# Feed-forward weights loaded a step ahead and let through by TensorE's progress, row norms from the accumulators, tiles of their own in the first batch

## The chip, the cores and the metric

The program runs on one core of one Trainium2 chip. The metric is device microseconds (us) of one execution, lower is better. Before the change three runs took 1228.06, 1234.43 and 1236.42 us, so the median is 1234.43 us.

Engines in the profile: PE is TensorE's matmul stream, PEld its weight loads, DVE is VectorE, ACT ScalarE, POOL GpSimd, SP SyncE. SP and POOL issue the kernel's DMAs. Each engine takes its own instructions strictly in order, so an instruction that waits holds up all that stand behind it on its engine.

## The reference

One decoder layer on x of 4 x 512 x 512 (batch, tokens, features) in float32:

```python
q = (ln(x) @ Wq + bq).reshape(B, T, 128, 16)   # k and v alike
att = softmax(q^T k / sqrt(128))               # per head 128 x 128: tokens are summed over
y = (att @ v).reshape(B, 512, 2048) @ Wo + bo  # per head 128 x 512
x = x + y
x = x + gamma * xattn(ln(x), ctx, ctx)         # 8 heads of 64 features, softmax over 512
w = clip(round(w / mean|w|), -1, 1) * mean|w|  # for w1, w3, w2 (1365 x 512)
x = x + (silu(ln(x) @ w1^T) * (ln(x) @ w3^T)) @ w2^T
```

Weights come as kernel inputs, so the quantization to three values is part of the computation: the mean of the absolute values of a whole matrix has to be known before any entry of it can be rounded.

## The kernel before, in words

**Attention, four rounds a batch.** Because an attention matrix sums over tokens, the kernel forms the Gram matrix `G = xn^T xn` of a batch once (`gram_upper`, `gram_rest`; matmuls `pg`, `gt`), and then runs rounds j = 0 to 3, each of four heads g = 0 to 3. A round has four products of 512 x 512 x 512: u = xn · Wo_j (matmuls `pu`), y = G · Wk_j (`py`), m = Wv_j · u (`pm`) and the scores Wq_j · y (`sc`). After them come the softmax `e` (`scores`: reduce_max L437, L438, exp L442, scaling L453), its transpose (`turned`, matmuls `pe`) and the output (`output`, matmuls `po`), which adds into four accumulators `acc` of 128 x 512 (L468). The transpose and output of a round are issued in the middle of the next one. All matmuls write into eight banks of PSUM, handed out in turn: a bank is used again only when what reads it (the exp for a score bank) is done.

**The first batch** also prepares the weights. `first_weights` loads four raw chunks of 128 x 512 for each of o, k, v, q, subtracts the last row (L227) and adds the bias by a small DMA on POOL (L230). `keep_weights` splits a chunk into parts h, l and, in later rounds, d (L253, L255, L258) and stores them to DRAM from POOL (L244). The raw chunks of o and q share seven buffers (tag "raw"), those of k and v and the parts of o share the 18 tiles of pool `a_w`, and the parts of k and v share twelve (tag "part"). The scaling at L227 multiplies by `gate`, a value that is always 1.0 but is computed from a result of TensorE (`gate_of`, L208): it has no effect on the numbers and makes the instruction depend on that result. The kernel is put in order by a scheduler that works from priorities and its own estimates; a gate keeps it from placing an instruction too early in an engine's order. Batches 1 to 3 load the kept parts (`weights`; for batch 1, d of the early rounds is made at L273) into pool `a_w`.

**Beside batches 1 to 3** run two side jobs, advanced by `tick()` inside `products`: `quantize` goes over w1, w3 and w2 in pieces (12, 12 and 11), first summing absolute values (`abs_w`, L498), then comparing with the scale (`tern_w`, L521, L522) and storing to DRAM on SP's queue (L525); both passes load a piece through `staged` (two buffers) right before they use it. `cross(b - 1)` is the cross-attention of the batch before: it loads the rows of x_a (the stored accumulators) once for the row norms (`cs`, L550, L551) and once more for the work (`cx`, L558), then scores `xs`, softmax, transposes `xp`, and `xo`. The cross-attention of batch 3 runs beside the feed-forward part, with its DMAs on POOL's queue.

**The feed-forward part** (L836 on) is one dense stream of matmuls with the quantized weights resident.

What the change and the steps of the prediction touch are the pools (L133 to L137, L747 to L751), `first_weights`, `keep_weights`, `weights`, the gates (L709, L720, L726), `held` (L738 to L740), `staged`, `quantize_steps` and the head of `cross`.

Of the kernel before, what the change touches and what calls it, by code (L numbers as in the profile page):

```python
# [10 lines left out]
F32 = mybir.dt.float32  # L11
# [7 lines left out]
P = 128  # L19
# [18 lines left out]
def decoder_layer_kernel(  # L38
# [29 lines left out]
    x_a = [dram.tile([T, D], F32, name=f"x_a_{b}") for b in range(B)]  # L68
    x_c = [dram.tile([T, D], F32, name=f"x_c_{b}") for b in range(B)]

    kept_t = {
# [58 lines left out]
    def apool(name, bufs):  # L130
        return apools.enter_context(tc.tile_pool(name=name, bufs=bufs))

    x3p, xnp, g3p, u3p, wp = (  # L133
        apool("a_x3", 12), apool("a_xn", 4), apool("a_g3", 1), apool("a_u3", 12), apool("a_w", 18)
    )
    yp, stp, tp = apool("a_y", 5), apool("a_stage", 2), apool("a_t", 3)
    ep, mp, accp = apool("a_e", 1), apool("a_m", 4), apool("a_acc", 4)  # L137
# [43 lines left out]

    def wtile(name, dt=F32R):
        return wp.tile([P, GW], dt, tag="w", name=name)

    w_of = {"q": wq, "k": wk, "v": wv}
# [25 lines left out]
    def first_weights(n, j, first, gate):  # L211

        if n != "o":
            last = first.tile([P, GW], F32, tag="last", bufs=2, name=f"{n}_last_{j}")
            load(heads(last), of_heads(w_of[n][:, D - 1 : D, :], j).to_broadcast([P, NG, DH]))
        chunks = []
        for k in range(KC):
            name = f"{n}_raw_{j}_{k}"
            if n in "oq":
                t = first.tile([P, GW], F32, tag="raw", bufs=7, name=name)  # L220
            else:
                t = wtile(name, F32)
            if n == "o":
                load(t, by_group(wo[j * T : (j + 1) * T, :], k))
            else:
                load(heads(t), of_heads(w_of[n][:, ts(k, P), :], j))
                nc.vector.scalar_tensor_tensor(t, t, gate[0], last, ALU.mult, ALU.subtract)  # L227
                if k == KC - 1:
                    bias = bqkv[:, ts(KINDS.index(n), GW)].rearrange("(o g) c -> g o c", o=1)
                    nc.gpsimd.dma_start(heads(t[P - 1 :, :]), of_heads(bias, j))  # L230
            chunks.append(t)
        return chunks

    def keep_weights(n, j, chunks, first, gate):


        def part(p, k):
            name = f"{n}_{p}_{j}_{k}"
            if n == "o":
                return wtile(name)  # L240
            return first.tile([P, GW], F32R, tag="part", bufs=12, name=name)

# [19 lines left out]

    def weights(n, b, j):
        if n == "q":
            return [load(wtile(f"q_{b}_{j}_{k}", F32), kept_q[j][ts(k, P), :]) for k in range(KC)]
        tris = []
        for k in range(KC):
            tri = Tri(*(wtile(f"{n}{p}_{b}_{j}_{k}") for p in "hld"))
            make = b == 1 and not exact(n, 0, j)
            for p in "hl" if make else "hld":  # L270
                load(getattr(tri, p).bitcast(F32), kept[n, j, p][ts(k, P), :])
            if make:
                nc.vector.tensor_tensor(  # L273
                    tri.d, tri.l.bitcast(F32), tri.h.bitcast(F32), ALU.subtract
                )
                nc.gpsimd.dma_start(kept[n, j, "d"][ts(k, P), :], tri.d.bitcast(F32))
            tris.append(tri)
        return tris

    def products(name, lhs, rhs, done, tick):  # L280

        for pair in ((0, 1), (2, 3)):
# [19 lines left out]
            for i in pair:  # L302
                done(i, hs[i], pd[i])
            tick()

# [165 lines left out]


    third = (HID + 2) // 3

# [9 lines left out]
    def staged(src, name):  # L484
        r, n = src.shape
        return load(stp.tile([P, 512], F32, tag="stage", name=name)[:r, :n], src)

    def quantize_steps(name):

# [5 lines left out]
        nc.vector.memset(sums, 0.0)  # L495
        for i, (src, t) in enumerate(pieces):
            piece = staged(src, f"abs_{name}_{i}")
            nc.vector.tensor_reduce(  # L498
# [17 lines left out]
        yield  # L516
        for i, (src, t) in enumerate(pieces):
            piece = staged(src, f"tern_{name}_{i}")
            r, n = t.shape
            above = stp.tile([P, 512], BF16, tag="above", name=f"above_{name}_{i}")  # L520
            nc.vector.tensor_scalar(above[:r, :n], piece, s[:r, 0:1], None, ALU.is_gt)  # L521
            nc.vector.scalar_tensor_tensor(  # L522
                piece, piece, s[:r, 1:2], above[:r, :n], ALU.is_lt, ALU.subtract
            )
            load(t, piece)  # L525
            yield
# [8 lines left out]
    xscale = 1.0 / math.sqrt(XD)  # L535
    CROSS_STEPS = 2 * NC + 1 + NC * (2 * NC + 2)

    def cross(b, cx, cin, cpp, cpt):
# [6 lines left out]

        mv = small.tile([P, NC, 2], F32, tag="mvc", bufs=2, name=f"mv_c_{b}")
        for c in range(NC):
            yield
            yield
            t = load(cx.tile([P, D], F32, tag="x", name=f"cs_{b}_{c}"), x_a[b][ts(c, P), :])  # L550
            moments(mv[:, c, :], t, f"c_{b}_{c}")  # L551
        rstd = small.tile([P, NC], F32, tag="rstdc", bufs=2, name=f"rstd_cc_{b}")
        nc.vector.tensor_copy(rstd, rstd_of(mv, f"c_{b}"))
        yield
# [116 lines left out]
    for j in range(HG):  # L671
# [30 lines left out]
        else:  # L702
# [46 lines left out]
        cpools.enter_context(tc.tile_pool(name=n, bufs=k, side="right"))  # L749
        for n, k in (("c_x", 3), ("c_in", 2), ("c_p", 4), ("c_pt", 2))  # L750
    ]  # L751
    for b in range(1, B):
        G = gram_upper(b, xs)
        waiting[2] = turned(*waiting[:3])
        output(*waiting)
        side = Side(cross(b - 1, *cpool), CROSS_STEPS, TICKS + 6)

# [5 lines left out]
        for j in range(HG):  # L763
            u3 = values_out(b, j, x3, weights("o", b, j), tick)
            if j > 0:
                waiting[2] = turned(*waiting[:3])
            ys = keys_of(b, j, g3, weights("k", b, j), tick)
            if j > 0:
# [6 lines left out]
            ms = values_of(b, j, weights("v", b, j), u3, tick)  # L775
            e = scores(b, j, weights("q", b, j), ys)
            waiting = [b, j, e, ms, accs]
        side.rest()
    waiting[2] = turned(*waiting[:3])
    output(*waiting)  # L780
    quant.rest()
    apools.close()

# [152 lines left out]
```

## Time and profile before

| | us |
|---|---|
| median of three runs | 1234.43 |
| the profiled execution | 1231.67 |
| its span in the profile | 1229.4 |
| PE busy | 1184.3 (96%) |
| DVE busy | 777.5 (63%) |
| ACT busy | 448.5 (36%) |
| POOL busy | 140.9 (11%) |
| DMA moved | 257.20 MB, mean 209 GB/s |

The profiled execution took 2.3 us more than its span; what lies around the span is not in the trace. Busy is time in which an engine had an instruction under way. Idle time of PE is therefore 1229.4 - 1184.3 = 45.1 us in all. The page gives the clock that TensorE was granted as a share of full speed (PEclk): a busy PE at a lower clock does less. In a list of waits, "A <- B: 5.2, 1, 5.2" says that A stood idle until B had finished, 5.2 us in all, once, at longest 5.2 us. In a timeline the bracket at the end of a row is the idle time in front of the instruction and what ended it.

### The profile page before, as it was taken

The page shows a single profiled execution, that of the slowest core. Times are in us where ns is not written, and L with a number is a line of the kernel's source. Part 1 is how long each engine was busy: PE and PEld are TensorE (multiplying, and loading weights), DVE is VectorE, ACT ScalarE, POOL GpSimd, SP SyncE. Part 2 cuts the span into 40 slices and gives each one's busy share as a digit, 9 for nine tenths or more (in the row PEclk, how much of TensorE's full clock was granted, in tenths as well). Part 3 has the DMA queues.
Part 4 walks back from the last instruction along what each step waited for, and adds up shares of the span by engine and source line. Part 5 has one row for each costly group of instructions (what it writes and reads, how often), then busy time and mean ns, then how long its engine had stood idle before and what let it go on. Part 6 is the DMA issues. An engine that isn't in the chain of part 4 may idle for free.

```text
span 1229.4 us, 15851 instructions
## 1 busy us (share of the span) xinstructions
PE 1184.3 (96%) x5262; PEld 825.7 (67%) x5262; DVE 777.5 (63%) x1579; ACT 448.5 (36%) x946; POOL 140.9 (11%) x238
## 2 busy tenths in 40 slices
PE   7999889889999999999999999999999999999998
PEld 3456565567776666777676677777667766678786
DVE  6866958587586856666677557485847835634232
ACT  2221212235242433433343334243445826823020
POOL 2533533120000001000000010000001000000000
PEclk9999999889999999999999999999999999999999
DMA  9799897786778686866787696677963120030101
GB/s 286 269 314 319 299 297 258 226 281 228 241 239 286 203 299 232 282 214 231 241 297 243 211 318 226 214 273 266 342 231 113 43 94 9 9 106 6 61 9 52
DMA packets 154137, 257.20 MB, mean 209 GB/s; under 512 B 16068, under 2 KB 59124, under 8 KB 154056
## 3 DMA queue, kind: packets, MB, share of 16 engines
q1 hardware_dynamic: 139272, 208.97, 51.6%
q0 software_dynamic: 14784, 47.22, 10.2%
q8 instruction: 42, 0.69, 0.2%
q14 instruction: 39, 0.32, 0.1%
HBM read 193.22 MB, written 62.91 MB: 208 GB/s over the span
## 4 chain that ended last, share of the span: by engine, by line
PE 80%; DMA 8%; DVE 4%; issue 4%; POOL 1%; ACT 1%; SPq 1%; POOLq 0%; DVEq 0%; ACTq 0%
PE h L851 13%; PE y L878 7%; PE xs L575 5%; PE xo L619 5%; PE xp L106 4%; PE sc L429 4%; PE po L466 4%; PE pg L361 2%; PE pm L320 2%; PE pu L320 1%; PE py_1d L299 1%; PE py_3d L299 1%; DMA abs_w<-in_w1t_dram 1%; PE py L320 1%; PE py_1h L288 1%
## 5 line engine op out<-in xcount | busy, mean ns | idle before, releaser
L851 PE MATMUL h<-fxh,t 128*128 128x512 f32 (+1 forms) x352 | 140.5, 401 | 0.8 <-ACT fxh L116 0.8
L851 PE MATMUL h<-fxl,t 128*128 128x512 f32 (+1 forms) x352 | 138.3, 395 | 0.0
L587 ACT ACTIVATE p<-xs,xnmax 128x512 f32<-128x512 f32 x128 | 87.0, 687 | 80.6 <-DVE xnmax L582 41.3
L581 DVE TENSOR_REDUCE xnmax<-xs 128x1 f32<-128x512 f32 x128 | 84.1, 685 | 30.6 <-PE xs L575 30.6
L851 PEld LDWEIGHTS h<-fxh,t 128*128 128x128 f32 (+1 forms) x352 | 65.1, 185 | 20.0 <-issue 1.5
L851 PEld LDWEIGHTS h<-fxl,t 128*128 128x128 f32 (+1 forms) x352 | 65.1, 185 | 15.7
L575 PE MATMUL xs<-keys,qs 64*128 64x512 f32 x256 | 73.0, 641 | 1.3 <-DVE m L308 1.3
L878 PE MATMUL y<-t,gh 128*128 128x512 f32 (+1 forms) x176 | 69.5, 395 | 0.0
L878 PE MATMUL y<-t,gl 128*128 128x512 f32 (+1 forms) x176 | 68.9, 391 | 0.0
L106 PEld LDWEIGHTS xp<-ident,p 128*128 128x128 f32 x512 | 58.8, 140 | 13.2 <-issue 3.0
L106 PE MATMUL xp<-ident,p 128*128 128x128 f32 x512 | 66.5, 273 | 0.8 <-DVE u L308 0.8
L619 PE MATMUL xo<-pt,vals 128*64 128x512 f32 x256 | 63.3, 599 | 2.4 <-ACT pt L109 2.4
L862 DVE SCALAR_TENSOR_TENSOR gf<-h,scales_w,sl 128x512 f32<-128x512 f32 (+1 forms) x44 | 32.9, 748 | 48.3 <-PE h L851 39.9
L109 ACT COPY pt<-xp 128x512 f32<-128x512 f32 x96 | 53.4, 594 | 26.5 <-PE xp L106 26.5
L466 PE MATMUL po<-m,eT 128*128 128x512 f32 x128 | 60.3, 615 | 2.7 <-ACT eT L109 2.7
L599 DVE TENSOR_SCALAR p<-p,xrden 128x512 f32<-128x512 f32 x128 | 56.4, 483 | 3.3
L320 PE MATMUL pm<-u,v_raw 128*128 128x512 f32 x128 | 55.6, 592 | 0.0
L663 POOL TENSOR_TENSOR acc<-acc,bo_bc 128x512 f32<-128x512 f32 x16 | 21.1, 1338 | 289.9 <-DMA acc<-in_x_dram 238.6
L860 ACT ACTIVATE sl<-h,scales_w 128x512 f32<-128x512 f32 (+1 forms) x44 | 30.2, 688 | 63.1 <-PE h L851 62.9
L468 DVE SCALAR_TENSOR_TENSOR acc<-po,acc 128x512 f32<-128x512 f32 x64 | 42.6, 687 | 15.6 <-PE po L466 15.4
L442 ACT ACTIVATE e<-sc,nmax 128x128 f32<-128x128 f32 x64 | 22.7, 369 | 79.8 <-DVE nmax L438 79.8
L171 ACT ACTIVATE uh<-u 128x512 fp32r<-128x512 f32 x48 | 30.4, 633 | 49.9 <-DVE u L308 49.7
(262 smaller groups left out, 2545.5 us busy)
## 6 DMA issues: line engine op xcount, KB each, us to landing
oh<-kept_oh SPq DMA_DIRECT2D x48, 256.0 KB, 4.7
ol<-kept_ol SPq DMA_DIRECT2D x48, 256.0 KB, 5.0
kh<-kept_kh SPq DMA_DIRECT2D x48, 256.0 KB, 5.0
kl<-kept_kl SPq DMA_DIRECT2D x48, 256.0 KB, 4.7
vh<-kept_vh SPq DMA_DIRECT2D x48, 256.0 KB, 4.5
vl<-kept_vl SPq DMA_DIRECT2D x48, 256.0 KB, 5.1
q<-kept_q SPq DMA_DIRECT2D x48, 256.0 KB, 5.2
kd<-kept_kd SPq DMA_DIRECT2D x44, 256.0 KB, 4.8
```

What stands on the lines that cost most here:

```text
L106: nc.tensor.transpose(pt[:, ts(k, P)], src[:, ts(k, P)], ident)
L109: nc.scalar.copy(dst, pv)
L320: nc.tensor.matmul(p, lhsT=lhs(k)[:, ts(i, P)], rhs=rhs(k), start=(k == 0), stop=(k == 3))
L429: nc.tensor.matmul(sc[:, ts(g, DH)], lhsT=w[k][:, ts(g, DH)], rhs=ys[k][:, ts(g, DH)], start=(k == 0), stop=(k == KC - 1),)
L466: nc.tensor.matmul(po, lhsT=eT[:, g, :], rhs=ms[g], start=True, stop=True)
L575: nc.tensor.matmul(sc, lhsT=qs[rows, ts(m, P)], rhs=keys[rows, :], start=True, stop=True)
L581: nc.vector.reduce_max(nmax[:, j : j + 1], scs[j], axis=AX.X)
L587: nc.scalar.activation(p, scs[j], AF.Exp, bias=nmax[:, j : j + 1], scale=xscale, accum_out=den[:, j : j + 1],)
L599: nc.vector.tensor_scalar(ps[j], ps[j], rden[:, j : j + 1], None, ALU.mult)
L619: nc.tensor.matmul(po[rows, :], lhsT=vals[:, l, rows], rhs=pt[j][:, l, :], start=(l == 0), stop=(l == NC - 1),)
L851: nc.tensor.matmul(ph[:r, :], lhsT=t[:, k, i * P : i * P + r], rhs=fxT[j][:, k, :], start=(k == 0 and j == 0), stop=(k == KC - 1 and j == 1),)
L878: nc.tensor.matmul(py, lhsT=g[i][j][:r, ts(c, P)], rhs=t2[:r, i, :], start=(i == 0 and j == 0), stop=(i == NHC - 1 and j == 1),)
```

## The change

1. **First batch, tiles.** Every kind of raw chunk gets four buffers of its own (tags raw_o, raw_k, raw_v, raw_q), "last" has three, v's parts have six (tag "vpart") and k's keep twelve. The parts h and l of a split o go into pool `a_u3`, d into a tag "od".
2. **First batch, gates.** v waits for u of the same round instead of m of the round before; q waits for y of the same round instead of u.
3. **Pools.** `a_w` and `a_stage` (now three buffers) move from the start of the kernel to the other side of the memory and open only after the first batch's pool has closed, with waits tile by tile. `c_x` has two buffers instead of three, and `above` one. The two `held` tiles are gone.
4. **Quantization.** `ahead` loads piece i + 1 before it hands out piece i. `settle` lets a piece through: VectorE makes a 1.0 out of the newest copied matmul result (`recent`), GpSimd multiplies one column of the piece by it, and VectorE's real work on the piece thereby depends on both. The results are stored on POOL's queue instead of SP's.
5. **Row norms.** `row_norms` takes the moments from the accumulators in SBUF (tokens laid out four to a partition), puts mean and 1/std through a DRAM tensor of 512 x 2 (store L569, load L571) to get them in the layout of `cross`, and the 16 loads `cs` of 256 KB go away. For batch 3 this is done before the feed-forward part.

```diff
+norm_a = [dram.tile([T, 2], F32, name=f"norm_a_{b}") for b in range(B)]
...
 def first_weights(n, j, first, gate):
-            if n in "oq":
-                t = first.tile([P, GW], F32, tag="raw", bufs=7, name=name)
-            else:
-                t = wtile(name, F32)
+            t = first.tile([P, GW], F32, tag=f"raw_{n}", bufs=4, name=name)
...
 def keep_weights(n, j, chunks, first, gate):
         def part(p, k):
-            if n == "o":
-                return wtile(name)
-            return first.tile([P, GW], F32R, tag="part", bufs=12, name=name)
+            if n == "o" and exact(n, 0, j):
+                if p != "d":
+                    return u3p.tile([P, D], F32R, tag="u3", name=name)
+                tag, bufs = "od", 4
+            else:
+                tag, bufs = ("vpart", 6) if n == "v" else ("part", 12)
+            return first.tile([P, GW], F32R, tag=tag, bufs=bufs, name=name)
...
 # products, after a pair is done
+            recent[:] = [hs[pair[0]]]
             tick()
...
+    def settle(piece):
+        r = piece.shape[0]
+        one = small.tile([P, 1], F32, tag="one", name="one")
+        nc.vector.tensor_scalar(one, recent[-1][:, 0:1], 1.0, 1.0, ALU.max, ALU.min)
+        nc.gpsimd.tensor_tensor(piece[:, 0:1], piece[:, 0:1], one[:r, :], ALU.mult)
+
+    def ahead(pieces, name):
+        coming = None
+        for i, (src, t) in enumerate([*pieces, (None, None)]):
+            here, coming = coming, src is not None and (staged(src, f"{name}_{i}"), t, i)
+            if here:
+                settle(here[0])
+                yield here
...
 def quantize_steps(name):
-        for i, (src, t) in enumerate(pieces):
-            piece = staged(src, f"tern_{name}_{i}")
+        for piece, t, i in ahead(pieces, f"tern_{name}"):
...
-            load(t, piece)
+            nc.gpsimd.dma_start(t, piece)
...
+    def row_norms(b, accs):
+        queue = nc.gpsimd if b == B - 1 else nc.sync
+        mv = small.tile([P, NG, 2], F32, tag="mvc", bufs=2, name=f"mv_c_{b}")
+        for g in range(NG):
+            yield
+            yield
+            moments(mv[:, g, :], accs[g], f"c_{b}_{g}")
+        rstd = rstd_of(mv, f"c_{b}")
+        nc.vector.tensor_copy(mv[:, :, 1:2].rearrange("p c s -> p (c s)"), rstd)
+        queue.dma_start(norm_a[b].rearrange("(p g) s -> p g s", g=NG), mv)
+        norms[b] = small.tile([P, NC, 2], F32, tag="norms", bufs=2, name=f"norms_{b}")
+        queue.dma_start(norms[b], norm_a[b].rearrange("(c p) s -> p c s", p=P))
+        for _ in range(3):
+            yield
...
 def cross(b, cx, cin, cpp, cpt):
-        for c in range(NC):
-            yield
-            yield
-            t = load(cx.tile([P, D], F32, tag="x", name=f"cs_{b}_{c}"), x_a[b][ts(c, P), :])
-            moments(mv[:, c, :], t, f"c_{b}_{c}")
...
-            normalize(qs, xc, mv[:, c, 0:1], rstd[:, c : c + 1])
+            normalize(qs, xc, norms[b][:, c, 0:1], norms[b][:, c, 1:2])
...
 # first batch
-        gates["q"] = gate_of(us[3])
+        gates["v"] = gate_of(us[3])
...
-        gates["o"] = gates["k"] = gate_of(ys[3])
+        gates["o"] = gates["k"] = gates["q"] = gate_of(ys[3])
...
-        gates["v"] = gate_of(ms[3])
...
-            for i in range(2):
-                held = stp.tile([P, 512], F32, tag="stage", name=f"held_{i}")
-                nc.vector.tensor_copy(held[:, 0:1], ys[i][:, 0:1])
...
+    wpools = ExitStack()
+    wp, stp = (
+        wpools.enter_context(tc.tile_pool(name=n, bufs=k, side="right", reuse_waits="tile"))
+        for n, k in (("a_w", 18), ("a_stage", 3))
+    )
```

More of the change, by code (lines that the diff above doesn't have):

```diff
@@ L1 @@
+import itertools
 import math
@@ L131, in apool @@
         return apools.enter_context(tc.tile_pool(name=name, bufs=bufs))
[L133 to L136, printed above, removed]
+    x3p, xnp, g3p, u3p = apool("a_x3", 12), apool("a_xn", 4), apool("a_g3", 1), apool("a_u3", 12)
+    yp, tp = apool("a_y", 5), apool("a_t", 3)
     ep, mp, accp = apool("a_e", 1), apool("a_m", 4), apool("a_acc", 4)
@@ L180, in load @@
         return dst
-    def wtile(name, dt=F32R):
-        return wp.tile([P, GW], dt, tag="w", name=name)
     w_of = {"q": wq, "k": wk, "v": wv}
@@ L213, in first_weights @@
         if n != "o":
-            last = first.tile([P, GW], F32, tag="last", bufs=2, name=f"{n}_last_{j}")
+            last = first.tile([P, GW], F32, tag="last", bufs=3, name=f"{n}_last_{j}")
             load(heads(last), of_heads(w_of[n][:, D - 1 : D, :], j).to_broadcast([P, NG, DH]))
@@ L261, in keep_weights, with weights, wtile @@
         return tris
-    def weights(n, b, j):
+    def weights(n, b, j, wp):
+        def wtile(name, dt=F32R):
+            return wp.tile([P, GW], dt, tag="w", name=name)
         if n == "q":
@@ L470, in output @@
                 (nc.gpsimd if b == B - 1 else nc.sync).dma_start(by_group(x_a[b], g), accs[g])
+    recent = []
     third = (HID + 2) // 3
@@ L495, in quantize_steps @@
         nc.vector.memset(sums, 0.0)
-        for i, (src, t) in enumerate(pieces):
-            piece = staged(src, f"abs_{name}_{i}")
+        for piece, t, i in ahead(pieces, f"abs_{name}"):
             nc.vector.tensor_reduce(
@@ L516, in quantize_steps @@
         yield
-        for i, (src, t) in enumerate(pieces):
-            piece = staged(src, f"tern_{name}_{i}")
+        for piece, t, i in ahead(pieces, f"tern_{name}"):
             r, n = t.shape
-            above = stp.tile([P, 512], BF16, tag="above", name=f"above_{name}_{i}")
+            above = stp.tile([P, 512], BF16, tag="above", bufs=1, name=f"above_{name}_{i}")
             nc.vector.tensor_scalar(above[:r, :n], piece, s[:r, 0:1], None, ALU.is_gt)
@@ L535, in decoder_layer_kernel @@
     xscale = 1.0 / math.sqrt(XD)
-    CROSS_STEPS = 2 * NC + 1 + NC * (2 * NC + 2)
+    CROSS_STEPS = NC * (2 * NC + 2)
+    NORM_STEPS = 2 * NG + 3
+    norms = {}
+    def row_norms(b, accs):
[12 more added lines that the diff above has]
+            yield
     def cross(b, cx, cin, cpp, cpt):
@@ L544, in load @@
             return dst
-        mv = small.tile([P, NC, 2], F32, tag="mvc", bufs=2, name=f"mv_c_{b}")
-        for c in range(NC):
-            yield
-            yield
-            t = load(cx.tile([P, D], F32, tag="x", name=f"cs_{b}_{c}"), x_a[b][ts(c, P), :])
-            moments(mv[:, c, :], t, f"c_{b}_{c}")
-        rstd = small.tile([P, NC], F32, tag="rstdc", bufs=2, name=f"rstd_cc_{b}")
-        nc.vector.tensor_copy(rstd, rstd_of(mv, f"c_{b}"))
-        yield
         def prepare(c):
@@ L749, in decoder_layer_kernel @@
         cpools.enter_context(tc.tile_pool(name=n, bufs=k, side="right"))
-        for n, k in (("c_x", 3), ("c_in", 2), ("c_p", 4), ("c_pt", 2))
+        for n, k in (("c_x", 2), ("c_in", 2), ("c_p", 4), ("c_pt", 2))
     ]
+    wpools = ExitStack()
[3 more added lines that the diff above has]
+    )
     for b in range(1, B):
@@ L755, in decoder_layer_kernel @@
         output(*waiting)
-        side = Side(cross(b - 1, *cpool), CROSS_STEPS, TICKS + 6)
+        side = Side(
+            itertools.chain(row_norms(b - 1, waiting[4]), cross(b - 1, *cpool)),
+            NORM_STEPS + CROSS_STEPS,
+            TICKS + 6,
+        )
         def tick():
@@ L763, in decoder_layer_kernel @@
         for j in range(HG):
-            u3 = values_out(b, j, x3, weights("o", b, j), tick)
+            u3 = values_out(b, j, x3, weights("o", b, j, wp), tick)
             if j > 0:
                 waiting[2] = turned(*waiting[:3])
-            ys = keys_of(b, j, g3, weights("k", b, j), tick)
+            ys = keys_of(b, j, g3, weights("k", b, j, wp), tick)
             if j > 0:
@@ L774, in decoder_layer_kernel @@
                 x3 = parts_of(b + 1, xs)
-            ms = values_of(b, j, weights("v", b, j), u3, tick)
-            e = scores(b, j, weights("q", b, j), ys)
+            ms = values_of(b, j, weights("v", b, j, wp), u3, tick)
+            e = scores(b, j, weights("q", b, j, wp), ys)
             waiting = [b, j, e, ms, accs]
@@ L780, in decoder_layer_kernel @@
     output(*waiting)
+    for _ in row_norms(B - 1, waiting[4]):
+        pass
     quant.rest()
+    wpools.close()
     apools.close()
```

## The prediction

> **What bounds the kernel now.** I read the busy shares first, then the chain that ended last.
>
> ```profile
> PE 1184.3 (96%) x5262; PEld 825.7 (67%) x5262; DVE 777.5 (63%) x1579; ACT 448.5 (36%) x946; POOL 140.9 (11%) x238
> PE 80%; DMA 8%; DVE 4%; issue 4%; POOL 1%; ACT 1%; SPq 1%; POOLq 0%; DVEq 0%; ACTq 0%
> ```
>
> The kernel is bound by PE, and the change takes no matmul away. All that can be won is PE's idle time, 1229.4 - 1184.3 = 45.1 us, and the time that PE works at a lowered clock. So the next view is what PE waits for, in the span's first 300 us (total, times, longest):
>
> ```profile
> PE pg L361 <- DVE xn L338: 8.7, 1, 8.7
> PE pu_2d L299 <- ACT e L442: 5.2, 1, 5.2
> PE py_0h L287 <- DMA kh<-kept_kh: 4.1, 2, 2.2
> PE pe L106 <- DVE e L453: 3.3, 1, 3.3
> PE pu_3d L299 <- ACT e L442: 3.3, 1, 3.3
> PE py_2h L288 <- DVE k_l L255: 0.9, 1, 0.9
> PE py_3h L287 <- DVE u L308: 0.9, 1, 0.9
> PE py_1h L288 <- DVE gate L208: 0.8, 1, 0.8
> ```
>
> The 8.7 us is the start of the kernel, which the change leaves alone. The rest is some 19 us, all around the first batch. Later there is little: from 300 to 922 us (batches 1 to 3) PE was busy 613.01 of 622 us, from 922 to the end (feed-forward) 301.21 of 307.4.
>
> Next, stretches of time (window, length, busy PE, PEld, DVE, ACT, POOL, granted clock, DMA share, GB/s). First three stalls with what lies around them, then the stretches of lowered clock in them:
>
> ```profile
> 122.90:131.20 8.30, 3.10 (x8) 2.47 (x8) 6.99 (x17) 4.24 (x12) 4.00 (x8) 0.79 0.78 266
> 224.20:236.00 11.80, 7.79 (x20) 4.03 (x21) 7.42 (x17) 4.65 (x16) 0.51 (x1) 0.71 0.70 203
> 248.50:264.00 15.50, 11.30 (x35) 8.18 (x35) 14.34 (x30) 6.05 (x11) 3.08 (x4) 0.78 0.82 277
> ...
> 126.80:130.30 3.50, 2.17 (x5) 1.78 (x6) 2.19 (x6) 2.73 (x11) 1.02 (x2) 0.63 1.08 379
> 178.00:181.50 3.50, 3.50 (x12) 2.74 (x11) 0.86 (x2) 1.45 (x3) 0.08 (x1) 0.63 1.06 417
> 225.80:232.70 6.90, 4.49 (x8) 2.20 (x9) 4.08 (x11) 3.42 (x12) 0.00 (x0) 0.56 0.58 191
> 249.70:253.20 3.50, 2.71 (x6) 1.91 (x7) 3.50 (x7) 0.95 (x2) 1.28 (x1) 0.63 0.61 210
> 256.50:260.00 3.50, 3.50 (x11) 2.66 (x11) 3.19 (x8) 2.07 (x4) 0.54 (x1) 0.63 0.81 254
> ```
>
> The clock falls with each larger stall, so a stall costs its idle time and then about 0.37 to 0.44 of PE's busy time in such a stretch.
>
> **Who made PE wait.** PE's 5.2 us was for a bank of PSUM that still held scores, until the exp (L442) had read them. VectorE's timeline shows why the exp was late (last bracket: idle time before, and what ended it):
>
> ```profile
> 119.22 0.75 DVE L227 SCALAR_TENSOR_TENSOR k_raw<-k_raw,gate,k_last 128x512 f32<-128x512 f32 x1 [7.72 <-DMA k_raw<-in_wk_dram]
> 123.84 0.68 DVE L437 TENSOR_REDUCE nmax<-sc 128x4 f32<-128x512 f32 x1
> ```
>
> The scores had ended at about 113.6 us. VectorE stood 7.72 us at L227, for a raw chunk of k whose load SP had issued late, and their maximum (L437) stood in its queue behind that and other work on weights. In the next round it is the same: 9.31 us at L227 for k_raw, then the maximum at 174.41 us and PE's 3.3 us.
>
> **First batch: tiles and gates (parts 1 and 2).** With four buffers of its own for each kind, a chunk no longer waits for one of another kind. In the built order of the changed kernel SP's loads of the next round stand in the order of need (o, k, v, q), and each becomes free as soon as the same kind's buffer of the round before is read. From matmul times of this trace that is 15 to 25 us before VectorE wants them, against the 5 to 8 us that a 256 KB load took here. VectorE's part is then a sum: what stands ahead of the maximum are the passes L227, L253, L255, L258 (750, 480, 690, 690 ns a chunk) and gates (145 ns). Added from the last copy of y, the maximum comes at 113 to 115 us, and PE wants the bank at 121 to 122: 5 to 7 us of slack. In the fourth round VectorE is done 23 us after y, and the bank wanted after 30. So these go:
> - second stall: 5.2 idle + 0.37 x 2.17 us busy at the low clock = 6.0;
> - third: 3.3 + 0.37 x 3.5 = 4.6;
> - small waits for parts and gates (0.9, 0.9, 0.8 above, and 0.5, 0.3, 0.3 below them): 3.7.
>
> Together **-14.3**. What is late next are bias DMAs on POOL (2 KB, 1.6 to 8.4 us to land, median 4.4), at which VectorE already stood 5.6 us for k and 2.1 for v: that is the second rival.
>
> **End of the first batch (part 4's first pieces).** The stall of 3.33 us at the transpose waits for the scaling of e (L453). In front of it VectorE stood at L498, the sums over w1 (waits of 3.4, 1.0, 0.6, 0.8, 2.1 us), whose loads come right before their use. In the changed order the first sum stands behind that scaling. So the window 224.2 to 236 goes: 11.8 - 7.79 = 4.0 idle, and 0.44 x 5.2 us = 2.3 of clock: **-6.3**.
>
> **Entry to batch 1 (parts 3 and 5).** The window 248.5 to 264 holds 15.5 - 11.3 = 4.2 idle + 0.37 x (2.71 + 3.5) = 2.3 of clock, 6.5 in all: PE waits for kh, a load behind SP's other work. Here I expect a new wait instead. The norms now go store, landing, load, landing, and `prepare(0)` (needs the norms) stands on VectorE ahead of y's first totals and of v's d parts, which PE's pm waits for. Two small transfers in a row cost 3.2 to 16.8 us by the bias rows, median 8.8; on SP the loads of k and v stand among these same waits (the norms' load cannot be issued before their store has landed, and the rest of kh, vh and vl are behind it). The 16 re-reads of x_a (4 MB, on which VectorE stood 18.3 us in all) go away, but they only bind here. I take a stall of 9 us with its clock, between 4 and 15: **+2.5** (-2.5 to +8.5).
>
> **Batches 1 to 3 (part 4 otherwise).** 70 pieces each get a one-column operation on VectorE (145 ns, as the gates) and one on POOL. No such POOL operation is in the trace; the rows on either side are a one-column memset (0.1 us) and a full 128x512 tensor operation (1.34 us), and I take the nearer, some 0.2. VectorE often stands for POOL's answer directly, so a piece costs it 0.5 us or so, 35 us in all, against 207 idle us in 300 to 922. The loads a step ahead give back up to 12.0 + 10.3 + 7.8 + 7.1 + 6.1 + 5.3 = 48.6 us of VectorE's waits, idle time that PE did not see. SP loses its stores of t (it stood 59.8 us for them while PE ran dense) and gets new stands at `cx`, since two buffers wait for x_c's stores (2.7 us median). Net on PE: **+1.5**, between -4 (the 9 us of idle left there cannot shrink by more than about half, since half waits for ScalarE) and +8. The feed-forward part keeps its matmuls; POOL's shorter queue in front of it I cost at nothing, since eight banks, some 15 us of work, cover it.
>
> The Trainium skill, "SBUF — State Buffer", section "A bandwidth-pool intuition that's wrong", speaks against the stores on POOL: a DMA through GpSimd that takes 620 ns alone takes some 3100 beside a VectorE copy. Here POOL's DMA issues took 517 to 563 ns in the mean while VectorE was 67 to 84% busy. By the page, an estimate, 35 stores would be 2.5 us late each, 87 us on POOL, which has more idle time than that.
>
> The Trainium skill, "TensorE: Matmul & The Clock Gate", section "Part 1: The HAM clock gate", says that the clock falls after an idle window of about 3.4 us. In this trace it also fell to 0.63 around stalls of 2.2 us. By the page only the 5.2 us stall would cost clock, and the estimate of the gain would be some 4 us smaller.
>
> **Sum.** 1231.7 - 14.3 - 6.3 + 2.5 + 1.5 = **1215.1 us**. The profiled execution lies 2.8 us below the median of the three runs, 1234.4, and their spread is 8 us; I predict in the profiled execution's terms, since the span's reasons are from it. About 1% is what a measurement here can tell from no change.
>
> **Rivals.**
> - *Entry clears too.* Small transfers land in their shortest times (1.6 us), SP's row of loads is early enough, and the 6.5 us go as well, with the small gains in batches 1 to 3: 1231.7 - 14.3 - 6.3 - 4 - 2 = about 1205. For it: the norms need no 256 KB transfer. Against: they are two round trips in a row.
> - *Half of the first batch's gain.* VectorE stops standing for k_raw and stands for biases or for a part's buffer whose store has not landed. Then half of 14.3 returns: about 1222. For it: the bias waits of 4.8 us. Against: slack of 5 to 7 us.
> - *The chain through POOL reaches PE: slower.* `settle` puts VectorE behind POOL, and POOL's stores wait for VectorE. PE's matmul results are copied by VectorE too. The other items give about -18, so the break-even is 18/70 = 0.26 us of each piece reaching PE. At 0.5 us, 35 us: 1231.7 - 18 + 35 = about 1249. For it: PE in 300 to 922 has no slack but its banks, and a gate made from the newest result makes VectorE wait in its own order. Against: VectorE's 33% idle, and waits of up to 5.3 us at the same pieces now leave PE 98.6% busy.
> - *The gates don't hold what they say* and the loads stay late: 1231, no change. Against: the built order.
>
> **How the numbers follow.** Forecast (1209 to 1219) 0.46; entry clears (1200 to 1209) 0.16; half (1219 to 1228) 0.18; no change (1228 to 1236) 0.05; slower, through POOL 0.15. The range leaves out the slow case and the lowest part: 1202 to 1233. Bounds: faster by over 1% is below 1222: 0.46 + 0.16 + a third of the half case = 0.68; within 1% 0.17; slower by over 1% 0.15.
>
> **What would show it.** Right: no wait of pu_2d and pu_3d for e above 1 us, no stand of VectorE at L227 above 3 us, no transpose waiting for L453; a stand of VectorE for the norms near 250 us, and PE waiting there; PE in batches 1 to 3 still 98% busy. Wrong: PE waiting for VectorE's copies across batches 1 to 3 with POOL as the releaser, a first batch in which VectorE's maximum is late behind another wait, or a slower first u because of the loads' new order.

## The result

The changed kernel takes 1243.14 us (median of seven runs, 1240.47 to 1246.64), the kernel before 1234.43 us beside it. The ratio is 1.0078, with a 95% interval of 1.0051 to 1.0104: slower by 0.8%. Predicted were 1215 us, with 1202 to 1233 as the range and a chance of 0.68 for faster by over 1%. The time lies outside the range and on the other side of the kernel before. One execution of an experiment below, of e13, ran at a mean granted clock of 0.851 and took 1324.81 us; it counts in no ratio.

The first lines of the page of the changed kernel (busy time of each engine, then the chain that ended last) look like those of before:

```profile
PE 1192.0 (96%) x5262; PEld 829.5 (67%) x5262; DVE 785.2 (63%) x1639; ACT 447.1 (36%) x943; POOL 181.0 (15%) x341
PE 83%; DMA 7%; DVE 4%; SPq 2%; issue 2%; ACT 1%; POOL 1%; POOLq 0%; DVEq 0%; ACTq 0%
```

The span grew by 11.9 us, from 1229.4 to 1241.3. PE's idle time grew from 45.1 to 49.3 us (+4.2), and its busy time from 1184.3 to 1192.0 us (+7.7) for the same 5262 matmuls: it worked at a lowered clock for longer. The waits of PE over the whole run say where (total, times, longest):

```profile
PE pg L363 <- DVE xn L340: 8.6, 1, 8.6
PE xt_f L845 <- DVE xn_f L102: 6.7, 1, 6.7
PE po L468 <- DVE y L310: 5.8, 1, 5.8
PE xs L602 <- DVE qs L102: 3.4, 1, 3.4
PE pu_3d L300 <- ACT e L444: 3.2, 3, 1.4
...
PE pm_0d L300 <- DVE vd L274: 2.5, 1, 2.5
PE pu_0h L289 <- DMA ol<-kept_ol: 2.2, 1, 2.2
PE py_0h L288 <- DMA kh<-kept_kh: 2.1, 1, 2.1
PE pu_1h L289 <- DMA ol<-kept_ol: 1.7, 1, 1.7
```

The wait of pu_2d for e (5.2 us) and that of pe for e (3.3 us) are gone, and that of pu_3d in the first batch shrank from 3.3 to 1.4 us (the other two of its three waits, 1.9 us, lie in batches 1 to 3). In their place are three groups that were not there: po for y in the first batch, a row of waits for ol, kh and vd at the entry to batch 1, and xt_f and xs at the start of the feed-forward part.

A table by place is the best view of it: when did the same matmul start, against the kernel before? (In us, from the timelines; minus is ahead.)

| matmul | before, at | changed | e1 | e22 | e20 |
|---|---|---|---|---|---|
| first of batch 1's Gram matrix (pg) | 215.4 | -7.5 | -11.2 | -5.6 | -14.8 |
| first of batch 2's Gram matrix | 456.0 | -2.3 | -6.4 | -13.0 | -20.9 |
| first of batch 3's Gram matrix | 683.9 | -1.7 | -6.2 | -10.4 | -20.4 |
| first of the feed-forward part (h) | 922.8 | +7.2 | +2.8 | +0.3 | -18.0 |
| last of the feed-forward part (y) | 1225.2 | +11.8 | +8.8 | +4.4 | -18.1 |

The last three are experiments below; e20 is the fastest. The changed kernel leaves the first batch 7.5 us ahead, has lost most of that by the end of batch 1, and loses 13.5 us more from batch 3's Gram matrix to the end, most of it around the start of the feed-forward part.

### The profile page after: what moved, and what is told of

The parts are those of the page before. It is cut to its first block, busy times and chain, and to the rows that moved or that the text cites. A ratio compares the mean times of both kernels' runs of the same rounds, so it can differ in the third digit from the quotient of the medians.

```text
span 1241.3 us, 16143 instructions
## 1 busy us (share of the span) xinstructions
PE 1192.0 (96%) x5262; PEld 829.5 (67%) x5262; DVE 785.2 (63%) x1639; ACT 447.1 (36%) x943; POOL 181.0 (15%) x341
## 3 DMA queue, kind: packets, MB, share of 16 engines
q0 software_dynamic: 16928, 54.57, 11.6%
## 4 chain that ended last, share of the span: by engine, by line
PE 83%; DMA 7%; DVE 4%; SPq 2%; issue 2%; ACT 1%; POOL 1%; POOLq 0%; DVEq 0%; ACTq 0%
PE h L885 13%; PE y L912 7%; PE xs L602 5%; PE xo L646 5%; PE po L468 4%; PE sc L431 4%; PE xp L108 4%; PE pm L322 3%; SPq L179 2%; PE pg L363 2%; PE pu_2h L288 1%; PE py_2h L288 1%; PE pu_2d L300 1%; PE pu_2h L289 1%; PE py_2h L289 1%
## 5 line engine op out<-in xcount | busy, mean ns | idle before, releaser
L885 PE MATMUL h<-fxh,t 128*128 128x512 f32 (+1 forms) x352 | 143.6, 408 | 0.7 <-ACT fxh L118 0.7
L468 PEld LDWEIGHTS po<-m,eT 128*128 128x128 f32 x128 | 23.8, 195 | 40.9 <-issue 28.2
L363 PE MATMUL pg<-xn 128*128 128x512 f32 (+3 forms) x128 | 37.9, 453 | 8.6 <-DVE xn L340 8.6
```

The lines of the kernel that those rows point to most:

```text
L363: nc.tensor.matmul(pg[:, :n], lhsT=xs[g][:, ts(m, P)], rhs=xs[g][:, m * P :], start=(g == 0), stop=(g == NG - 1),)
L468: nc.tensor.matmul(po, lhsT=eT[:, g, :], rhs=ms[g], start=True, stop=True)
L885: nc.tensor.matmul(ph[:r, :], lhsT=t[:, k, i * P : i * P + r], rhs=fxT[j][:, k, :], start=(k == 0 and j == 0), stop=(k == KC - 1 and j == 1),)
```

## What the trace of the changed kernel says of each loss

**First batch.** VectorE's timeline (start, duration, engine, line, what; in the bracket the idle time before it), of the kernel before and then of the changed one:

```profile
94.41 0.69 DVE L85 BATCH_NORM_STATS2 st_a<-xn 128x6 f32<-128x512 f32 x1 [4.10 <-DMA xn<-in_x_dram]
```

```profile
80.36 0.21 DVE L205 TENSOR_SCALAR gate<-u 128x1 f32<-128x1 f32 x2 [0.85 <-ACT u L352]
92.20 0.69 DVE L87 BATCH_NORM_STATS2 st_a<-xn 128x6 f32<-128x512 f32 x1 [11.62 <-DMA xn<-in_x_dram]
...
97.11 1.28 DVE L310 SCALAR_TENSOR_TENSOR y<-py_1t,py_1d 128x512 f32<-128x512 f32 x2
```

VectorE stood 11.62 us for the loads of x of batch 1 (their row statistics stand at this place in the kernel before too, where the first of them waited for nothing and the second 4.10 us), and the copies of y, for which PE waited, stood behind. SP's timeline shows why the load came late:

```profile
77.18 7.42 SPq L179 DMA_DIRECT2D q_raw<-in_wq_dram  x4
85.08 1.67 SPq L179 DMA_DIRECT2D o_raw<-in_wo_dram  x1
86.86 0.37 SPq L179 DMA_DIRECT2D xn<-in_x_dram  x1
```

Four loads of q and one of o, which now go out as early as their own buffers allow, stand in SP's queue ahead of it. In the kernel before the first of these loads went out at 76.74 us, and the longest stand for one was 4.1 us.

**Entry to batch 1.** SP's waits between 205 and 300 us, of the kernel before and of the changed one:

```profile
SPq L179 <- DMA abs_w<-in_w1t_dram: 11.3, 6, 3.4
SPq L179 <- DVE sums_w L498: 10.5, 7, 7.1
```

```profile
SPq L179 <- DVE sums_w L517: 40.3, 8, 15.3
```

SP stood 40.3 us for a buffer of the quantization that VectorE's sum (L517) had to release, with oh, ol, kh, kl, vh and vl behind it; before, the pieces had cost it 21.8 us, 10.5 for VectorE's sum and 11.3 for a piece's landing. From 300 to 900 us it stood another 118.9 us for the landing of quantized pieces, since the next piece goes into their buffer (before, 26.1 us, and 59.8 us for the stores of t, which are now POOL's):

```profile
SPq L179 <- DMA t_w<-tern_w: 118.9, 24, 9.5
SPq L179 <- DVE sums_w L517: 32.3, 6, 6.4
```

**Start of the feed-forward part.** Three queues. VectorE: the moments of the last accumulators (st_c) now stand ahead of the statistics of xn_f, which PE needs first; and qs stands for the norms.

```profile
920.98 0.66 DVE L87 BATCH_NORM_STATS2 st_c<-acc 128x6 f32<-128x512 f32 x1
...
921.64 0.66 DVE L87 BATCH_NORM_STATS2 st_f<-xn_f 128x6 f32<-128x512 f32 x1
...
925.07 1.92 DVE L102 TENSOR_SCALAR xn_f<-xn_f,mv_f,rstd_f 128x512 f32<-128x512 f32 x4
...
939.09 0.55 DVE L102 TENSOR_SCALAR qs<-cx,norms 128x512 f32<-128x512 f32 x1 [8.40 <-DMA norms<-norm_a]
```

In the kernel before, the statistics of xn_f were done between 876.7 and 879.6 us, over 40 us ahead of the first h:

```profile
876.70 0.68 DVE L85 BATCH_NORM_STATS2 st_f<-xn_f 128x6 f32<-128x512 f32 x1
```

POOL waits for each small transfer:

```profile
929.17 0.54 POOL L569 DMA_DIRECT2D norm_a<-mv_c  x1
936.58 0.76 POOL L571 DMA_DIRECT2D norms<-norm_a  x1 [6.86 <-DMA norm_a<-mv_c]
```

And SP, of the kernel before and then of the changed one:

```profile
886.10 26.37 SPq L179 DMA_DIRECT2D t<-t_w  x26
```

```profile
888.40 10.10 SPq L179 DMA_DIRECT2D t<-t_w  x17
914.96 0.32 SPq L580 DMA_DIRECT2D x_c<-cx  x1
919.06 8.47 SPq L179 DMA_DIRECT2D t<-t_w  x11
```

Eleven loads of w2's quantized weights (ten of 256 KB, one of 170) go out only at 919 us, when x_a and the norms have to pass. The tile lies on other memory than before, because `a_w` and `a_stage` moved to the other side: what lies there now is in use up to batch 3's last output (`po`), for which SP waits right before these loads (from its waits between 885 and 935 us):

```profile
SPq L179 <- PE po L468: 3.7, 1, 3.7
```

The stretch 920 to 940 us, before and changed (length, busy PE, PEld, DVE, ACT, POOL, granted clock, DMA share, GB/s):

```profile
920.00:940.00 20.00, 19.17 (x91) 15.57 (x90) 13.69 (x32) 9.67 (x14) 6.16 (x12) 1.00 0.63 200
```

```profile
920.00:940.00 20.00, 10.23 (x38) 8.31 (x40) 10.33 (x27) 4.90 (x8) 2.91 (x5) 0.74 0.84 282
```

## Experiments

Each is timed against the kernel before on the same chip. "Against the changed kernel" is the difference of the two ratios times 1233 us. Lengths of a stage ("batch 1" is from its first matmul pu to the Gram matrix of batch 2) are from the one profiled execution of each kernel.

### e1: batch 1's row statistics held back (theory A)

```diff
+        if late is not None:
+            for g in range(NG):
+                nc.vector.tensor_scalar(xs[g][:, 0:1], xs[g][:, 0:1], late, None, ALU.mult)
         mv = small.tile([P, NG, 2], F32, tag="mv", name=f"mv_a_{b}")
...
-            xs = normed(1, False)
+            xs = normed(1, False, gates["v"][0])
```

> The changed kernel, with the row statistics of batch 1's x (L87, st_a) held back by a value that is 1.0 and comes from u of the fourth round, so that VectorE does not stand for their loads at 80 to 92 us. Theory A (that stand of 11.6 us made PE wait 5.8 + 1.3 us and lowered the clock for some 3 us' worth): about 10 us faster than the changed kernel, near 1233 us, with no wait of po for y above 2 us before 120 us. Rival (the parts of v and k are late anyway, since their gates now open at u and y of their own round): 1240 us or more, with a wait of similar size in its place.

Measured: 1233.49 us, ratio 1.0000 (0.9980 to 1.0021), 9.6 us faster than the changed kernel. The wait of po for y is gone. What is left in the first batch between 60 and 204 us:

```profile
PE pu_2d L300 <- ACT e L447: 3.2, 1, 3.2
PE sc L434 <- DVE o_l L253: 0.7, 1, 0.7
```

Theory A holds. The 3.2 us that are left have the cause that the prediction had as its second rival: VectorE stands 7.53 us for a bias of k, and the maximum of the scores comes behind it. VectorE's passes are through at 114.1 us, so without that stand the maximum would have come at about 114.5 us, an estimate, inside the prediction's 113 to 115.

```profile
121.64 0.49 DVE L251 TENSOR_SCALAR k_h<-k_raw,gate 128x512 fp32r<-128x512 f32 x1 [7.53 <-DMA k_raw<-in_bqkv_dram]
122.04 0.68 DVE L442 TENSOR_REDUCE nmax<-sc 128x4 f32<-128x512 f32 x1
```

The profiled execution was the slowest of the ten (1240.03), so the table's lead at the end is too small for this kernel.

### e5: the old gates (part 2 undone)

```diff
-        gates["v"] = gate_of(us[3])
+        gates["q"] = gate_of(us[3])
...
-        gates["o"] = gates["k"] = gates["q"] = gate_of(ys[3])
+        gates["o"] = gates["k"] = gate_of(ys[3])
...
+        gates["v"] = gate_of(ms[3])
```

> The changed kernel with part 2 undone: v waits for m of the round before and q for u of the same round, as before the change. Theory A (the stand at 80 to 92 us is for the loads of batch 1's x, whatever VectorE does before it): po still waits 4 to 6 us for y, the time stays within 3 us of the changed kernel, 1240 to 1246 us. Rival (the later gates left VectorE with nothing to do ahead of that stand, and so cost the first batch): v's passes then stand ahead of it, the wait of po goes, 1234 to 1238 us.

Measured: 1249.83 us, ratio 1.0120 (1.0088 to 1.0151), 5.2 us slower than the changed kernel by the ratios (the intervals overlap a little); neither expectation gave that. PE between 60 and 204 us:

```profile
PE pu_2d L300 <- ACT e L444: 5.4, 1, 5.4
PE po L468 <- DVE y L310: 4.8, 1, 4.8
PE py_1d L300 <- ACT e L444: 1.1, 1, 1.1
```

po waits as expected of theory A, whatever stands ahead. But the late exp of the kernel before (pu_2d for e, 5.2 us there) is back. With the old gate VectorE's work on v stands ahead of the maximum again, and VectorE waits for its load:

```profile
127.55 0.75 DVE L221 SCALAR_TENSOR_TENSOR v_raw<-v_raw,gate,v_last 128x512 f32<-128x512 f32 x1 [4.75 <-DMA v_raw<-in_wv_dram]
...
130.59 0.68 DVE L439 TENSOR_REDUCE nmax<-sc 128x4 f32<-128x512 f32 x1
```

Tiles of their own alone do not free the score bank in time; part 1 needs part 2. The other way round, part 2 without part 1, was not run.

### e2, e11, e12: the start of the feed-forward part (theories B and D)

e2 takes the norms of batch 3 from reloaded rows again. e11 exchanges two pools:

```diff
-    f1, fxb, f3, fx, f2, fwk, fg = (
-        fpool("f_w1", 1), fpool("f_xb", 1), fpool("f_w3", 1), fpool("f_x", 2), fpool("f_w2", 1),
+    f1, fxb, f3, f2, fx, fwk, fg = (
+        fpool("f_w1", 1), fpool("f_xb", 1), fpool("f_w3", 1), fpool("f_w2", 1), fpool("f_x", 2),
```

e12 does both.

> The changed kernel, with the row norms of batch 3 alone taken as before the change (reloaded rows, inside the cross-attention); those of batches 0 to 2 stay with the accumulators. Theory B (the moments of the last accumulators stand ahead of the first feed-forward normalization in VectorE's queue, and the round trip of the norms through DRAM makes the first xs late: 6.7 + 3.4 us of PE and some 7 us' worth of clock): about 13 us faster, near 1230 us, feed-forward start as before, PE dense there. Rival (the feed-forward part starts late because its weights t and x_c land late, with POOL and SP changed around it): 1240 us or more and xt_f still waiting.

> The changed kernel, with two pools of the feed-forward part exchanged in memory, so that the tile of w2's quantized weights lies on memory that batch 3 leaves early. Theory D (since a_w and a_stage moved away, that tile lies on memory that the last output uses; its 11 loads stand on SP until 919 us and fill the DMA just when x_a and the norms have to go through it): the loads are issued by 900 us, the norms land earlier, the 3.4 us of xs for qs go, some 4 to 6 us faster, 1237 to 1239 us; the 6.7 us of xt_f stay, since VectorE's order stays. Rival (the round trip of the norms is long by itself): 1241 us or more, xs still waiting for qs.

> The exchange of the two pools and, beside it, the row norms of batch 3 as before the change. Theory B and D together (VectorE's order makes xt_f late, the 11 loads make the first xs late): both waits go, the start of the feed-forward part is as before, 12 to 15 us faster, 1228 to 1231 us. Rival (one more cause there): 1235 us or more.

Measured: e2 1243.22 us, ratio 1.0088 (1.0067 to 1.0108), no gain; e11 1237.35, 1.0037 (1.0017 to 1.0058), 5.1 us faster than the changed kernel by the ratios (the intervals overlap a little); e12 1233.36, 1.0006 (0.9985 to 1.0026), 8.9 us faster. Expected of e12 were 12 to 15.

Theory B alone falls with e2: xt_f no longer waits, as it said, but VectorE stands longer for the reloaded rows (cs), which meet the eleven loads in the DMA, and xs waits 7.8 us in place of 3.4:

```profile
937.49 0.69 DVE L87 BATCH_NORM_STATS2 st_c<-cs 128x6 f32<-128x512 f32 x1 [12.17 <-DMA cs<-x_a]
```

In e11 the loads of t went out by 911 us, the norms' store landed in 3.4 us (6.9 in the changed kernel), and xs does not wait any more; the 6.8 us of xt_f stay, as theory D said. In e12 both are gone. So there are two causes, and each hides part of the other: repairing VectorE's order alone moves the wait to the DMA. From the Gram matrix of batch 3 to the first h e12 still takes 242.4 us (247.8 in the changed kernel, 238.9 before); where these 3.5 us lie was not followed. Behind the first h it is as fast as the kernel before.

### e3, e6: the quantization's loads at the entry (theory C)

e3 loads a piece right before its use again (three buffers, no `settle`, stores on SP). e6 starts the quantization 18 calls of `tick()` later.

> The changed kernel, with the quantization as before the change: a piece is loaded right before its use into one of three buffers, no value of PE lets it through, and the results are stored from SP's queue. Theory C (at the entry to batch 1 SP stands for the buffers that VectorE's late sums release, 20.4 us in all, and ol, kh and vl are late behind it): the waits for ol and kh of 225 to 276 us shrink, 3 to 6 us faster, 1237 to 1240 us. Rival 1 (the loads a step ahead pay in batches 1 to 3): 1246 us or more. Rival 2 (nothing of part 4 reaches PE): 1242 to 1244 us.

> The changed kernel, with the quantization started a round later: its first piece after 18 of the 72 calls of tick() in batch 1, the pieces then closer together. Theory C: SP is free of it at the entry, ol, kh and vl come earlier, 4 to 8 us faster, 1235 to 1239 us. Rival (SP stands for x_a's stores and the accumulators there anyway): 1241 us or more.

Measured: e3 1243.15 us, ratio 1.0079 (1.0056 to 1.0102), the same as the changed kernel, as its second rival said; e6 1245.82, 1.0116 (1.0088 to 1.0144), 4.7 us slower by the ratios (the intervals overlap), a miss. But e3's equal time is no proof that nothing of part 4 reaches PE. In its profiled execution batch 1 took 227.4 us, against 232.0 in the changed kernel, which is what theory C expects; the next two stages, up to the first h, took 4.8 us more and ate it up. Why they did stays open. In e6 SP's stand for VectorE's sums did not go, it moved: 81.0 us between 205 and 900 us. Both leave the loads of the pieces in SP's queue, so neither tests theory C cleanly. That needed an experiment that takes SP's stand away.

### e13, e14: repairs together

e13 joins e1, e11 and e2. e14 takes, beside that, all row norms from reloaded rows as before the change.

> The changed kernel with three repairs: batch 1's row statistics held back, the two pools exchanged, the row norms of batch 3 as before the change. If their effects add (about 6 to 10 us in the first batch, 12 to 15 us at the feed-forward part), 1220 to 1225 us, 0.988 to 0.992 of the kernel before. If the first batch's gain is lost at the entry to batch 1: 1228 us or more.

> As the run with three repairs, but the row norms of all four batches as before the change, with two buffers. Theory E (my step for the entry to batch 1: the norms' round trip costs PE a new stall there): some 3 to 8 us faster than the run with three repairs, and xs waits no longer for qs in batches 1 to 3. Rival (SP's row of loads and weights, not the norms, sets the entry): the same within 3 us, or slower by the re-reads.

Measured: e13 1227.74 us, ratio 0.9947 (0.9929 to 0.9964), less than expected. e14 1223.97, 0.9922 (0.9901 to 0.9942). The effects add to 16.2 and 19.2 us against the changed kernel. Between the two the intervals overlap, so this pair does not settle what the norms of batches 0 to 2 cost.

### e15, e16, e20: part 4 on top of e14

e15 has the quantization of before (as e3), e16 only lacks `settle`, e20 loads the pieces from POOL's queue:

```diff
-        return load(stp.tile([P, 512], F32, tag="stage", name=name)[:r, :n], src)
+        piece = stp.tile([P, 512], F32, tag="stage", name=name)[:r, :n]
+        nc.gpsimd.dma_start(piece, src)
+        return piece
```

> Parts 1 to 3 alone, repaired: the kernel with batch 1's row statistics held back, the two pools exchanged and all row norms as before the change (1224.0 us), with the quantization as before the change too. Theory C (part 4 makes SP stand at the entry to batch 1, but its loads ahead pay about as much later): the entry loses 5 to 8 us less of PE, batches 1 to 3 some 4 to 6 us more, in all within 3 us, 1221 to 1227 us. Rival 1 (part 4 pays): 1228 us or more. Rival 2 (part 4 costs): 1220 us or less.

> The same repaired kernel (1224.0 us), with the loads a step ahead but without the value that lets a piece through: no operation of VectorE and GpSimd for it, 70 fewer on each. By my step for batches 1 to 3 (0.4 us of VectorE a piece, under its idle time) that operation costs PE nothing: within 3 us, unless the order that it holds is worth something. Then VectorE's passes over the pieces stand ahead of their loads and PE waits for its copies: 1228 us or more. If the chain through POOL reaches PE, my slower rival: 1219 us or less.

> The same repaired kernel (1224.0 us), with the loads of the quantization's pieces from POOL's queue, so that SP no longer stands for a piece's buffer (33.8 us between 205 and 300 us in the run with three repairs). Theory C: oh, ol, kh and vh come earlier at the entry to batch 1, PE loses 5 to 8 us less there: 1216 to 1220 us. Rival (PE waits there for x_a, the accumulators and the DMA's throughput, not for SP's stands): within 2 us of 1224. Slower, if POOL's stands delay the stores of od, kd and vd and with them VectorE: 1227 us or more.

Measured: e15 1218.50 us, ratio 0.9870 (0.9836 to 0.9904); e16 1227.19, 0.9940 (0.9919 to 0.9960); e20 1212.35, 0.9825 (0.9801 to 0.9849). e20 is 12.0 us faster than e14 with one line changed, more than expected, and the fastest kernel of this study: 1.75% faster than before. Batch 1 took 220.8 us in it, 231.2 in e14. PE's waits between 205 and 300 us in e20:

```profile
PE py_0h L288 <- DMA kh<-kept_kh: 5.0, 1, 5.0
PE po L471 <- ACT eT L111: 0.7, 1, 0.7
PE pm_0d L300 <- DVE vd L274: 0.5, 1, 0.5
PE pu_0h L289 <- DMA ol<-kept_ol: 0.3, 1, 0.3
```

One stall instead of a row of them, and SP's stands for sums are gone from its list. Theory C holds: what the queue costs falls where it said. The edit also changes when the pieces' loads share the DMA with the weights, and that part was not separated; the bytes are the same (257.2 MB). Where SP issues the loads, part 4 costs (e15 against e14: 6.4 us gained by undoing it, its second rival and not what I expected; the intervals just touch, and batch 1 took 224.5 us against 231.2). `settle` itself is free within what these runs tell (e16 against e14: intervals overlap).

### e21, e22, e23: what was still open

e22 is that one line in the changed kernel, e23 in the kernel before; e21 is e20 with the norms of batches 0 to 2 from the accumulators.

> The changed kernel with one edit: the pieces of the quantization are loaded from POOL's queue, not SP's. Theory C (in the changed kernel SP stands for a piece's buffer, and everything behind it in SP's queue is late, at the entry to batch 1 and in batches 1 to 3): 8 to 13 us faster, 1229 to 1235 us, the waits at the feed-forward part as before (6.7 and 3 us). Rival (that queue costs only where the first batch and the feed-forward part are repaired already): 1239 us or more.

> The run with pieces loaded from POOL (1212.4 us), but the row norms of batches 0 to 2 from the accumulators, as the change has them; batch 3 as before the change. Theory E (the norms' two small transfers make a new stall at the entry, my step of 2.5 us): 2 to 6 us slower, 1215 to 1219 us. Rival (they cost nothing once SP is free): within 2 us of 1212.

> The kernel before the change, with the pieces loaded from POOL's queue and nothing else changed. If SP's stands for the pieces cost PE in the kernel before too (10.5 us for sums between 205 and 300 us, 60 us for the quantized pieces later): 3 to 6 us faster, 0.995 to 0.9975. If they are hidden there, since a piece is loaded right before its use: within 2 us, and the cost belongs to the change.

Measured: e22 1234.04 us, ratio 1.0002 (0.9982 to 1.0022), 9.4 us faster than the changed kernel: SP's queue is by itself the third cause, of about the size of the other two, and batch 1 took 219.4 us instead of 232.0. e21 1214.91, 0.9854 (0.9820 to 0.9888), 3.6 us slower than e20 by the ratios, as theory E expected, but the intervals overlap, and the place is not the one it names: batch 1 took 220.2 us in e21 and 220.8 in e20. e23 1271.97, 1.0313 (1.0271 to 1.0355), 3% slower, which nothing forecast. There PE waits in batches 1 to 3 for VectorE's copies:

```profile
PE po L466 <- DVE y L308: 10.7, 2, 5.7
PE xs L577 <- DVE pt L111: 6.8, 1, 6.8
PE xs L577 <- DVE m L308: 6.8, 1, 6.8
```

Without `settle`, and with the loads one right before each use, POOL holds a load back once for 91.0 us, and other work of POOL stands behind it. That this is how VectorE's copies come late was not tested by itself. It says that the move to POOL is no gain in general; it paid in the two kernels that have part 4. Which piece of part 4 it needs was not tested.

## Why the prediction was wrong

Three steps failed, in the order of what they cost: the feed-forward part, put at 0 (+13.5 us); the entry to batch 1, put at +2.5 (+11.3); and the first batch, put at -14.3 (-7.5).

- **First batch, -14.3.** Half of it came. The stand that the step is about went: VectorE no longer stands for k_raw (19.2 us of it between 60 and 204 us before, none now), and the two stalls behind the score bank fell from 5.2 and 3.3 us to none and 1.4. What failed is the step "What is late next are bias DMAs". Late next was a load of x for batch 1, behind loads of weights that now go out early. The sum of VectorE's passes begins at the last copy of y, and this stand lies ahead of that copy: it was 4.1 us before, 11.6 now, and is in no term. The biases came after it, as the second rival had them: in the changed kernel VectorE stood 3.98 us for one right ahead of the maximum of the third round, and PE waited 1.4; in e1, where x no longer held things up, 7.53 us used up the slack of 5 to 7 us and PE waited 3.2. The lead at the Gram matrix of batch 1 is 7.5 us instead of 14.3; with the stand for x removed, 11.2 in e1, 12.7 in e13 and 14.8 in e20. So the size of the term was about right; what it lacked was the load of x, and in e1 the bias.
- **End of the first batch, -6.3.** Held: the wait of pe for e at this place is gone, and from the Gram matrix to the first u of batch 1 PE needs 13.8 us where it needed 19.9, -6.1. (The sum's 0.44 x 5.2 us takes more busy time than the 4.49 us of its row; it makes 2.0 us, not 2.3.)
- **Entry to batch 1, +2.5.** The sign was right, the mechanism wrong and the size too small: from its first u to the Gram matrix of batch 2, batch 1 took 232.0 us where it had taken 220.7, +11.3, of which 4.8 are idle time of PE and 6.5 more busy time for the same work, at a clock of 0.96 instead of 0.98. VectorE does not stand for the norms: qs at 249.53 us has no idle time before it. What PE waits for are ol, oh, kh and vd, and the reason is SP's stand for buffers of the quantization (40.3 us). The prediction read SP's waits as something that PE does not see, since SP had stood 59.8 us for stores of t while PE ran dense. But that was in batches 1 to 3, where weights are loaded with room to spare; at the entry the weights have none. With that queue relieved, batch 1 takes 219.4 us in e22 and 220.8 in e20, and the whole is 9.4 and 12.0 us shorter. The norms' round trip, which the step priced, shows no cost there: 220.2 us in e21, which has it.
- **Batches 1 to 3, +1.5.** Nearly right: PE was busy 98.35, 97.81, 100.00, 97.88 and 100.00 us in the five 100 us from 300 to 800 us (98.77, 96.88, 100.00, 98.14 and 99.21 before). Batch 2 took 228.6 us, 227.9 before. The slower rival, the chain through POOL, did not come: VectorE waited 46 times for POOL's answer, 0.42 us each, PE's waits from 300 to 900 us came to 6.0 us in all, and e16, which has no such chain, was not faster than e14:

```profile
DVE sums_w L517 <- POOL abs_w L497: 9.8, 19, 1.3
DVE above_w L539 <- POOL tern_w L497: 9.5, 27, 1.0
```

  The one-column operation took 0.18 to 0.19 us in the median, as taken.
- **Feed-forward part, 0.** This is the step that cost most: +13.5 us from batch 3's Gram matrix to the end. "POOL's shorter queue in front of it I cost at nothing, since eight banks, some 15 us of work, cover it" looked at one queue and at matmuls already running. It missed that the moments of the accumulators can only come after the last output, that the scheduler puts them ahead of xn_f's statistics on VectorE (6.7 us), and that moving two pools changes which memory a later tile takes over, and so when its loads may start (with the norms' round trip, 3.4 us). The lowered clock after these stalls comes on top.

A sum by stage, from the timelines of the two profiled executions: -7.5 us up to the Gram matrix of batch 1, -6.1 from there to the first u, +11.3 in batch 1, +0.7 in batch 2, +8.9 from the Gram matrix of batch 3 to the first h and +4.6 behind it make +11.9 us, the growth of the span (by the ratio, which takes in the other executions too, it is 9.6). Predicted were -14.3 and -6.3, then +4.0 for the entry and batches 1 to 3 together, and 0. Both new costs come of what goes out early or lies elsewhere: a load that is issued sooner takes the place of another load in a queue, and a pool that moves gives a later tile other memory to wait for.

Of the Trainium skill's rules that the prediction weighed, the one on DMAs through GpSimd ("SBUF — State Buffer", section "A bandwidth-pool intuition that's wrong": some 3100 ns beside a VectorE copy) did not show: the 35 stores of quantized pieces took POOL 558 ns each in the median, 652 at the most. The operations of VectorE in the rows above are other ones than a copy, so the page's own case was not tested. The one in "TensorE: Matmul & The Clock Gate", section "Part 1: The HAM clock gate", ties the low clock to an idle window of about 3.4 us. Here the 2.14 us wait of py_0h, up to 240.17 us, was followed by a clock of 0.58 between 241.5 and 245 us, while the 2.17 us wait of pu_0h, up to 227.97 us, was followed by 1.00. So a shorter wait was followed by a low clock too, but not each was.

## What to carry to other kernels

When loads are allowed to go out earlier, list for each queue what they now stand in front of, and ask for each of those whether its use has slack where it is used, not on average over the run. Where a pool moves, look at which later tile inherits its memory and when its last reader ends. A stage that the change seems not to touch (here the last one) gets its own line in the sum: an operation that can only start after the last output stands there ahead of something.

## What the runs showed of the hardware

A store of 4 KB to DRAM took 6.9 us to land while the eleven loads of w2's weights were under way, and 3.4 us in e11, where they had gone earlier: the same store took twice as long beside that traffic. After the stall of 6.7 us PE's granted clock was 0.50 from 926 to 933 us, in which PE was busy 6.3 us. At full clock that work would have taken half of it, an estimate: 3.2 us on top, half as much again as the stall. The one-column operation on POOL took 0.18 us at the least and 0.63 at the most.
